# Denominators of a softmax convolution by TensorE tiles of 128 rows and 32 columns, and the gate's small matmuls in the products' tile shape

## The chip, the core and the metric

The kernel runs on one core of a Trainium2 chip. The metric is the device time of one execution in microseconds. Before the change the median of three runs is 2595.57 us.

## The reference, cut to what matters

The input has 16 images of 256 channels, 28 x 28 pixels. After a group norm two convolutions follow, each with a lookup in place of the full product, and then a squeeze-and-excitation gate:

```python
def amm_conv3x3(x, centroids, w_sub, stride=1):
    ...
    d = jnp.sum(p * p, axis=-1)[..., None] - 2.0 * jnp.einsum('bncs,cks->bnck', p, centroids) + jnp.sum(centroids * centroids, axis=-1)[None, None]
    attn = jax.nn.softmax(-d, axis=-1)
    lut = jnp.einsum('cks,cso->cko', centroids, w_sub)
    out = jnp.einsum('bnck,cko->bno', attn, lut)
...
def se_layer(x, w1, b1, w2, b2):
    s = jnp.mean(x, axis=(2, 3))
    s = jax.nn.relu(s @ w1 + b1)
    s = jax.nn.sigmoid(s @ w2 + b2)
    return x * s[:, :, None, None]
```

Two parts are touched here. The softmax has for each channel and pixel a denominator, the sum of 16 exponentials. The gate has two small matrix products for each image: 256 to 16 (the hidden layer) and 16 to 256.

## The kernel before, in words

All arithmetic is float32. The kernel does not build the big table. For each channel it first makes, from the 16 exponentials, nine weighted means (one for each tap of the 3 x 3 patch), and then multiplies these with the convolution's weights. Work goes by blocks: two layers, 16 images, and in each image four blocks (half of the channels, half of the rows of pixels), 128 blocks in all. A block has 392 pixels.

For each block TensorE does four things:

- **logits** (L607, matmuls at L616, tile `lg`): distances, by tiles of 32 rows and 32 columns, sixteen of which fill the array. They come in four portions `mm` of 16 matmuls. ScalarE turns each portion into exponentials (tile `e`, L627).
- **num_b** (L675, matmuls at L681, tile `nb`): for all four portions, a sum over the 16 exponentials of a channel with the ninth tap's centroid values (a numerator), and the plain sum (the denominator). It uses tiles of 64 rows and 32 columns. In the loop, `mm` is outermost, then the four column groups `i`, then the two row halves `r`. Row half 0 writes bank 0 of a pair of PSUM banks and row half 1 bank 1, and each bank accumulates over the four portions.
- **num_a** (L661, matmuls at L667, tile `na`): the other eight numerators, also by tiles of 64 rows and 32 columns.
- **product** (L747, matmuls at L752, tile `acc`): nine matmuls with two column halves each, by tiles of 128 rows and 64 columns (the constant `AW` is 64). The products of four blocks are combined by differences, so that seven groups of weights do the work of eight.

Rows of `nb`: in each group of 32 rows, channels that belong to row half 0 have their numerator in rows 0 to 15 and their denominator in rows 16 to 31, and the other half the other way round. `rows_of` (L84) gives the two row numbers. `split_r` (ScalarE, L691) and `join_r` (VectorE, L695) gather the denominators from the two banks into one tile `r` with the masks `m_hi` and `m_lo`; `split_q` and `join_q` (L699, L704) do the same with the numerators. `recip_dve` (L708) inverts `r`, and `spread` (L717) copies the reciprocals to the rows of each numerator with a shuffle, whose pattern is given by `mask_of` (L711). VectorE or GpSimd then multiplies (L743, L732), and GpSimd makes the differences (`mix`, L757, L761).

The order of TensorE's work is written out by hand: each job has a step number and a position, and they are sorted. In steady state there are two steps for each block, one after the other: logits, num_b, logits, a product; then logits, num_a, logits, a product. So TensorE changes from one tile shape to another four times in each step. SP's queue carries the loads of the patches (`patches`, L587, L594) for later blocks, and among them single loads of tables.

Small matmuls stand at fixed places behind a product. The group norm's (`by_cols`, L532, L534, tile `gnp`) are already done as two matmuls of 128 rows and 64 columns. The gate's hidden layer, `se_hidden` (L1038, matmuls at L1045, tile `sep`), multiplies the channel sums of an image with `w1_sb`, whose 32 columns hold the 16 hidden units twice: tiles of 128 rows and 32 columns. ScalarE adds the bias (L1047) and writes the hidden units into two columns, one for each half of the output channels (`halves`, L1049). `se_gate` (L1051, matmul at L1053) multiplies these 32 rows with `w2_sb`: one matmul of 32 rows and 128 columns. Each runs once for each of the 16 images. In the first 15 images the hidden layer is at step `g + 14` and the gate at `g + 17`, behind the product of that step, with `g` the image's first step; the last image has both at the end. The tables of the gate are loaded by `load_se` (L249, six DMAs on SP's queue) at step 92, behind the build of a table on GpSimd (`prep_cwb`, L998).

Of the kernel before, what the change touches and what calls it, by code (L numbers as in the profile page):

```python
# [8 lines left out]
F32 = mybir.dt.float32  # L9
I32 = mybir.dt.int32  # L10
U32 = mybir.dt.uint32
AF = mybir.ActivationFunctionType
ALU = mybir.AluOpType
# [4 lines left out]
P = 128  # L18
# [5 lines left out]
N = RT * W  # L24
# [56 lines left out]
AW = 64  # L81


def rows_of(m, c, a):  # L84
    r, c4, mm = c >> 1, 2 * (c & 1) + a, m & 3
    return r, c4, mm, 16 * r + 4 * mm + c4, 16 * (1 - r) + 4 * mm + c4


@with_exitstack
def kernel(  # L90
# [22 lines left out]
    nc = tc.nc  # L113
    B, C, _ = x.shape
    NB = C // P
    RED = se_w1.shape[1]

    const = ctx.enter_context(tc.tile_pool(name="const", bufs=1))
    dram = ctx.enter_context(tc.tile_pool(name="dram", bufs=1, space=DRAM))
    small = ctx.enter_context(tc.tile_pool(name="small", bufs=2))  # L120
# [12 lines left out]
    def fixed(u, kind):  # L133
        return None if u["step"] is None else EARLY.get((kind, u["step"] // 2))

    def banks(name, step=None, role=None, tag=None):
        if tag is not None:
            pass
        elif step is None:
            spin[0] = (spin[0] + 1) % 4  # L140
            tag = spin[0]
        else:
            tag = (role - step // 2) % 4
        return p_ring.tile([P, 2, 512], F32, tag=f"ps{tag}", name=name)

    def bank(name, step=None, role=None, tag=None):
        return banks(name, step, role, tag)[:, 0, :]

    def after(u, n):
        return None if u["step"] is None else u["step"] + n  # L150
# [44 lines left out]
    def load(ap, name, eng=None):  # L195
        t = const.tile(list(ap.shape), ap.dtype, name=name)
        (eng or nc.sync).dma_start(t, ap)
        return t

    wts = {}  # L200
# [37 lines left out]
        (nc.gpsimd if n in ("S2", "S4") else nc.vector).tensor_tensor(wl[n], wl[a], wl[b], op)  # L238

    vecs = load(vec, "vecs", nc.gpsimd)  # L240
    w1_sb = const.tile([P, NB, 2 * RED], F32, name="w1_sb")
    w2_sb = const.tile([2 * RED, P], F32, name="w2_sb")
    b1_sb = const.tile([2 * RED, 1], F32, name="b1_sb")
    halves = const.tile([2 * RED, NB], F32, name="halves")
    nc.gpsimd.memset(halves, 0.0)
    nc.gpsimd.memset(halves[:RED, 0:1], 1.0)
    nc.gpsimd.tensor_scalar(halves[:, 1:2], halves[:, 0:1], -1.0, 1.0, op0=ALU.mult, op1=ALU.add)

    def load_se():  # L249
        for k in range(NB):  # L250
            nc.sync.dma_start(w1_sb[:, :, k * RED : (k + 1) * RED], se_w1.rearrange("(b p) r -> p b r", p=P))
            nc.sync.dma_start(w2_sb[k * RED : (k + 1) * RED], se_w2[:, k * P : (k + 1) * P])
            nc.sync.dma_start(b1_sb[k * RED : (k + 1) * RED], se_b1.rearrange("(p o) -> p o", o=1))
# [80 lines left out]
    def small_bank(name, step, tag=None):  # L334
        return bank(name, step, step and ROLES["small"][step % 2], EARLY["small"].get(step) if tag is None else tag)
# [196 lines left out]
    def by_cols(ps, lhsT, rhs):  # L532
        for o in range(0, P, AW):
            nc.tensor.matmul(ps[o : o + AW], lhsT=lhsT[:, o : o + AW], rhs=rhs, start=True, stop=True)  # L534
# [140 lines left out]
    def num_b(u):  # L675
        bs = banks("nb", after(u, 2), ROLES["nb"], fixed(u, "nb"))
        for mm in range(4):
            es = u["e", mm]
            for i in range(4):
                for r in range(2):  # L680
                    nc.tensor.matmul(  # L681
                        bs[32 * i : 32 * i + 32, r, :N],
                        lhsT=wts["cwb", u["hh"]][64 * r : 64 * r + 64, mm, i, :],
                        rhs=es[64 * r : 64 * r + 64, i, :],
                        start=(mm == 0), stop=(mm == 3),
                    )
        u["nb"] = bs

    def split_r(u):
# [21 lines left out]
    def mask_of(k):  # L711
        if k == 8:
            return [(xx + 16) % 32 for xx in range(32)]
        mm, r = divmod(k, 2)
        return [16 * (1 - r) + 4 * mm + (xx >> 3) for xx in range(32)]

    def spread(u, mm):  # L717
        if mm == 4:
            rb = rpool.tile([P, N], F32, tag="rb1", name="rb1", bufs=1)
            nc.vector.stream_shuffle(rb, u["r"], mask_of(8))  # L720
        else:
            rb = rpool.tile([P, 2, N], F32, tag="rb", name="rb", bufs=4)
            for r in range(2):
                nc.vector.stream_shuffle(rb[:, r, :], u["r"], mask_of(2 * mm + r))  # L724
        u["rb", mm] = rb
# [310 lines left out]
    se = {}  # L1036

    def se_hidden(b, step=None, tag=None):  # L1038
        ysum = ys[b, "sum"]
        ps = small_bank("sep", step, tag)[: 2 * RED, :1]  # L1040
        terms = [(k, ysum[:, k, i : i + 1]) for k in range(NB) for i in range(2 if b >= B - 1 else 1)]
        if (b, "rest") in ys:
            terms += [(k, ys[b, "rest"][:, k : k + 1]) for k in range(NB)]
        for n, (k, term) in enumerate(terms):
            nc.tensor.matmul(ps, lhsT=w1_sb[:, k, :], rhs=term, start=n == 0, stop=n == len(terms) - 1)  # L1045
        hid = small.tile([2 * RED, 1], F32, name="se_hid")
        nc.scalar.activation(hid, ps, AF.Relu, bias=b1_sb, scale=1.0 / HW)  # L1047
        se[b] = small.tile([2 * RED, NB], F32, name="se_hh")
        nc.scalar.activation(se[b], halves, AF.Copy, scale=hid)  # L1049

    def se_gate(b, step=None, tag=None):  # L1051
        ps = small_bank("sep", step, tag)[:, :NB]
        nc.tensor.matmul(ps, lhsT=w2_sb, rhs=se[b], start=True, stop=True)  # L1053
        gt = small.tile([P, NB], F32, name="se_gt")
        for k in range(NB):
            nc.scalar.activation(
                gt[:, k : k + 1], ps[:, k : k + 1], AF.Exp, bias=nb2_sb[:, k : k + 1], scale=-1.0
            )
        nc.scalar.activation(gt, gt, AF.Identity, bias=one, scale=1.0)
        se[b] = gt  # L1060
# [179 lines left out]
    for j, u in enumerate(blocks):  # L1240
        gi, g = 8 * (j // 4), 2 * j
        for mm in range(5):
            kind = "one" if mm == 4 else "pair"
            t = g + 1 + (j > 2) if mm == 4 else g + 2 + (j > 1)
# [9 lines left out]
    for j, u in enumerate(blocks):  # L1254
# [3 lines left out]
        for p in range(2):  # L1258
# [6 lines left out]
            for q in range(2):  # L1265
                mm = 2 * p + q
# [11 lines left out]
        kept = () if j == 1 else SLOT_MM[1 : 4 if wide_next(j) or j == 0 else 2 : 2]  # L1278
        g = 2 * j + 1 + (j > 2)
        at(g, 1.0, num_b, u)  # L1280
        at(g, 1.05, split_r, u)
        at(g, 1.2 if j > 1 else 1.055, join_r, u)
# [21 lines left out]
    for l in range(2):  # L1304
        for b in range(B):
# [33 lines left out]
            if n == 2 * B - 1:  # L1339
# [14 lines left out]
                at(g + 11, 1.91, norm_out, l, b, *c22)  # L1354
                at(g + 11, 1.96, rest_sum, b, 1)
                at(g + 11, 1.98, se_hidden, b, None, 1)
                at(g + 11, 1.995, se_gate, b, None, 1)
                at(g + 12, 0.0, norm_join, b, (n, 11))
                at(g + 12, 0.01, se_recip, b)
# [39 lines left out]
            else:  # L1399
# [5 lines left out]
                if not last:  # L1405
                    at(g + 14, 2.1, se_hidden, b, g + 14)
                    at(g + 17, 2.1, se_gate, b, g + 17, 2 if near else None)
                    at(g + 18, 0.3, se_recip, b)
                    for q in range(NB):
                        if near:  # L1410
                            at(*((g + 19, 1.95) if q else (g + 18, 0.35)), gate_wide, b, q)
                            at(*((g + 19, 1.965) if q else (g + 18, 0.36)), finish_wide, b, q)
                            at(*((g + 19, 1.965) if q else (g + 18, 0.36)), store, b, q)
                            continue
                        at(g + 18, 1.9, finish_gate, b, q)
                        at(g + 20, 0.05, finish_sum, b, q)
                        at(g + 20, 1.9, finish_relu, b, q)
                        at(g + 20, 2.2, finish_add, b, q)
                        at(g + 20, 2.25, store, b, q)
# [21 lines left out]
    for o in range(2):  # L1441
# [7 lines left out]
        for part in range(2):  # L1449
            c = 40 + 8 * o + 2 * part  # L1450
# [5 lines left out]
    for part in range(3):  # L1456
        c = (68, 70, 76)[part]
# [7 lines left out]
    for part in range(4):  # L1465
        at((84, 84, 91, 92)[part], (0.5, 1.5, 2.3, 1.5)[part], prep_cwb, part)
    at(92, 2.7, prep_keep, d_cwb)
    at(92, 2.3, load_se)
    for n in range(3):
        at(96 + 8 * n, 2.6, sums_load, 3 * n)  # L1470
# [23 lines left out]
    ps = bank("gnq", tag=3)  # L1494
# [59 lines left out]
    with tc.If(rv > 0):  # L1554
        with tc.For_i(0, B, 1) as it:
            t = io.tile([P, NB, HW], F32, tag="xt", name="xt")
# [13 lines left out]
            for l in range(2):  # L1570
# [6 lines left out]
                for t2 in range(2):  # L1577
                    us = []
                    for hh in range(2):
                        u = {"l": l, "b": B, "t": t2, "hh": hh, "w": 0, "step": None}  # L1580
# [32 lines left out]
                if l == 0:  # L1613
                    for o in range(NB):
                        for r in range(2):
                            to_home2(B, o, r)
            se_hidden(B)
            se_gate(B)
            se_recip(B)
            for k in range(NB):  # L1620
# [108 lines left out]
```

## Time and profile before

| | |
|---|---|
| three runs | 2591.88, 2595.57, 2597.56 us |
| the profiled execution | 2593.79 us |
| its span, first to last instruction | 2592.0 us |
| TensorE busy | 2574.5 us |
| GpSimd, VectorE, ScalarE busy | 1911.3, 1777.4, 1372.3 us |
| granted clock of TensorE | 1.00 |

The profile is of one execution. A page of it gives busy time, the chain of work that ended last, and groups of instructions by line. A row of a group has the line, the engine, the operation, the written and the read tile, the tile shape on the array (rows\*columns), the count, the busy time, the mean length of one and the idle time before the group. Of TensorE's two rows PE is the matmuls and PEld the loads of weights. A float32 matmul stands in the records as two, so 32 matmuls of num_b are 64 instructions. Matmuls on different tiles of the array overlap, and the ends of matmuls are modelled; starts are measured. The timeline merges neighbours of the same line into one row: its start, its length from the first start to the last end, and the count.

### The profile page before, as it was taken

How to read it: one execution, taken by the hardware profiler on the slowest of the kernel's cores; microseconds unless marked ns; L12 is line 12 of the kernel's file. 1: busy time of each engine (PE TensorE's matmuls, PEld its weight loads, DVE VectorE, ACT ScalarE, POOL GpSimd, SP SyncE). 2: the span in 40 equal slices, each digit the busy share in tenths (PEclk: the TensorE clock that was granted, in tenths of full speed). 3: DMA queues.
4: the chain of work that ended last, by engine and by line, in shares of the span. 5: the costliest groups of instructions: out<-in, count | busy, mean ns of one | idle time of the engine just before them, and what ended most of it. 6: DMA issues, size and time to landing. Idle time of an engine off the chain costs nothing.

```text
span 2592.0 us, 94062 instructions
## 1 busy us (share of the span) xinstructions
PE 2574.5 (99%) x41146; PEld 1079.9 (42%) x41146; DVE 1777.4 (69%) x3797; ACT 1372.3 (53%) x1913; POOL 1911.3 (74%) x1341
## 2 busy tenths in 40 slices
PE   8999999999999999999999999999999999999998
PEld 3444444444444444444444444444444444444444
DVE  8766656666567666566676767766776667767676
ACT  6445444445445445444545555555555655555665
POOL 7687666776568776667676887878878788787786
PEclk9999999999999999999999999999999999999999
DMA  7556656665555575664664445444445444444442
GB/s 230 169 129 181 200 163 185 166 171 166 165 146 144 161 196 175 168 178 129 175 170 104 114 109 130 118 122 121 103 123 130 117 117 113 116 124 129 117 105 67
DMA packets 213321, 372.59 MB, mean 144 GB/s; under 512 B 29497, under 2 KB 183529, under 8 KB 212329
## 3 DMA queue, kind: packets, MB, share of 16 engines
q1 hardware_dynamic: 206584, 333.75, 48.3%
q0 software_dynamic: 6176, 32.66, 3.5%
q8 instruction: 327, 5.36, 0.9%
q14 instruction: 90, 0.73, 0.1%
q10 hardware_dynamic: 144, 0.10, 0.0%
HBM read 288.46 MB, written 77.95 MB: 141 GB/s over the span
## 4 chain that ended last, share of the span: by engine, by line
PE 97%; ACT 1%; POOL 1%; DVE 1%; issue 0%; DMA 0%; POOLq 0%; ACTq 0%
PE acc L752 52%; PE lg L616 17%; PE na L667 14%; PE nb L681 14%; ACT e L627 0%; POOL qp L761 0%; ACT pt L1139 0%; PE sep L1053 0%; POOL qp L732 0%; PE sep L1045 0%; DMA xt<-in_x 0%; DVE qp L743 0%; PE tap L393 0%; PE sqp L375 0%; POOL qo L732 0%
## 5 line engine op out<-in xcount | busy, mean ns | idle before, releaser
L752 PE MATMUL acc<-qp,wall 128*64 128x392 f32 x6176 | 1088.2, 494 | 1.5 <-POOL qp L761 1.2
L627 ACT ACTIVATE e<-lg 128x784 f32<-128x784 f32 x960 | 738.0, 821 | 626.5 <-PE lg L616 623.6
L761 POOL TENSOR_TENSOR qp<-qp,qp 128x784 f32<-128x784 f32 x512 | 946.2, 1871 | 148.4 <-DVE qp L743 147.9
L752 PEld LDWEIGHTS acc<-qp,wall 128*64 128x64 f32 x6176 | 424.4, 137 | 626.9 <-issue 532.0
L724 DVE STREAM_SHUFFLE rb<-r 128x392 f32<-128x392 f32 x1024 | 553.2, 607 | 0.0
L616 PE MATMUL lg<-pt,wd 32*32 32x392 f32 x15872 | 468.2, 499 | 0.5 <-issue 0.5
L695 DVE SCALAR_TENSOR_TENSOR r<-nb,kst,r 128x392 f32<-128x392 f32 x128 | 80.1, 626 | 443.8 <-ACT r L691 443.8
L667 PE MATMUL na<-e,cwa 64*32 64x392 f32 x8192 | 374.8, 492 | 0.4 <-issue 0.4
L681 PE MATMUL nb<-e,cwb 64*32 64x392 f32 x8192 | 374.7, 492 | 0.2 <-ACT e L627 0.2
L743 DVE TENSOR_TENSOR qp<-na,rb 128x784 f32<-128x784 f32 x352 | 333.9, 972 | 58.5 <-PE na L667 45.5
L732 POOL TENSOR_TENSOR qo<-qo,rb 128x392 f32<-128x392 f32 x128 | 133.0, 1039 | 289.8 <-DVE rb L720 289.6
L709 DVE RECIPROCAL r<-r 128x392 f32<-128x392 f32 x128 | 333.2, 2603 | 4.4
L732 POOL TENSOR_TENSOR qp<-qp,rb 128x784 f32<-128x784 f32 x160 | 296.8, 1865 | 2.9
L681 PEld LDWEIGHTS nb<-e,cwb 64*32 64x32 f32 x8192 | 190.7, 106 | 174.8 <-issue 21.0
L667 PEld LDWEIGHTS na<-e,cwa 64*32 64x32 f32 x8192 | 182.4, 106 | 183.9 <-issue 74.2
L616 PEld LDWEIGHTS lg<-pt,wd 32*32 32x32 f32 x15872 | 116.3, 103 | 276.7 <-issue 233.6
L752 PE MATMUL acc<-qp,w_A 128*64 128x392 f32 x1024 | 181.1, 495 | 0.0
L691 ACT ACTIVATE r<-nb,kst 128x392 f32<-128x392 f32 x128 | 86.8, 678 | 163.2 <-PE nb L681 160.1
L752 PE MATMUL acc<-qo,wall 128*64 128x392 f32 (+1 forms) x772 | 159.3, 491 | 0.1
L651 POOL TENSOR_TENSOR z<-z,mx 128x1568 f32<-128x1568 f32 x32 | 91.9, 2871 | 91.4 <-DVE mx L645 91.0
L737 ACT COPY qp<-na 128x784 f32<-128x784 f32 x160 | 130.0, 813 | 22.6 <-PE na L667 21.1
L759 POOL TENSOR_TENSOR qo<-qo,qo 128x392 f32<-128x392 f32 x128 | 131.6, 1028 | 0.1
(241 smaller groups left out, 1621.3 us busy)
## 6 DMA issues: line engine op xcount, KB each, us to landing
pt<-home SPq DMA_DIRECT2D x744, 209.0 KB
pt<-home SPq DMA_DIRECT2D x744, 104.5 KB
home<-xpad SPq DMA_DIRECT2D x30, 899.0 KB
xt<-in_x SPq DMA_DIRECT2D x30, 784.0 KB
out_dram<-y SPq DMA_DIRECT2D x31, 392.0 KB
pt<-in_p SPq DMA_DIRECT2D x6, 784.0 KB
d_wS<-st SPq DMA_DIRECT2D x12, 192.0 KB
wall<-d_wS SPq DMA_DIRECT2D x4, 576.0 KB
```

The lines of the kernel that those rows point to most:

```text
L616: nc.tensor.matmul(bk[32 * c : 32 * c + 32, :N].rearrange("p (r w) -> p r w", w=W), lhsT=(wx[u["hh"]] if early(u) else wts["wd", u["hh"]]) ...
L627: nc.scalar.activation(eg[:, 2 * i : 2 * i + 2, :], bk[:, :, :N], AF.Exp, scale=2.0)
L667: nc.tensor.matmul(bs[32 * i : 32 * i + 32, r, :N], lhsT=wts["cwa", u["hh"]][64 * r : 64 * r + 64, mm, i, :], rhs=es[64 * r : 64 * r + 64, ...
L681: nc.tensor.matmul(bs[32 * i : 32 * i + 32, r, :N], lhsT=wts["cwb", u["hh"]][64 * r : 64 * r + 64, mm, i, :], rhs=es[64 * r : 64 * r + 64, ...
L709: nc.vector.reciprocal(u["r"], u["r"])
L724: nc.vector.stream_shuffle(rb[:, r, :], u["r"], mask_of(2 * mm + r))
L732: nc.gpsimd.tensor_tensor(q, q, u.pop(("rb", mm)), ALU.mult)
L737: nc.scalar.copy(pair(u, mm), u.pop(("na", mm))[:, :, :N])
L743: nc.vector.tensor_mul(pair(u, mm), u.pop(("na", mm))[:, :, :N], rb)
L752: nc.tensor.matmul(accs[key][o : o + AW, : cols[1] - cols[0]], lhsT=wl[w][:, k, o : o + AW], rhs=us["q", k][:, cols[0] : cols[1]], start=f ...
L759: nc.gpsimd.tensor_tensor(out_u["q", 8], in0["q", 8], in1["q", 8], ALU.subtract)
L761: nc.gpsimd.tensor_tensor(pair(out_u, mm), pair(in0, mm), pair(in1, mm), ALU.subtract)
```

## The change

`num_b` uses tiles of 128 rows and 32 columns: both row halves in one matmul, 16 matmuls for a block in place of 32. Bank 0 now accumulates portions 0 and 1, and bank 1 portions 2 and 3. So that no two channels get the same row, the row numbers are dealt out anew (`rows_of`), and the shuffle patterns follow (`mask_of`).

The gate's tables are padded with zeros. `w1_sb` has 64 columns for each half of the channels, so the hidden layer's matmuls are 128\*64. `w2_sb` has 128 rows, and the hidden units stand in two fixed tiles of 128 rows in place of pool tiles of 32; the gate is done by `by_cols`, two matmuls of 128\*64. Five fills on GpSimd clear these tiles ahead of the loads in `load_se`. The room that GpSimd's DMA descriptors take in SBUF is set to 4096 bytes for each partition, which moves the tiles' addresses.

```diff
 def rows_of(m, c, a):
     r, c4, mm = c >> 1, 2 * (c & 1) + a, m & 3
-    return r, c4, mm, 16 * r + 4 * mm + c4, 16 * (1 - r) + 4 * mm + c4
+    rn = 8 * mm + 2 * c + a
+    return r, c4, mm, rn, (rn + 16) % 32
...
-    w1_sb = const.tile([P, NB, 2 * RED], F32, name="w1_sb")
-    w2_sb = const.tile([2 * RED, P], F32, name="w2_sb")
-    b1_sb = const.tile([2 * RED, 1], F32, name="b1_sb")
-    halves = const.tile([2 * RED, NB], F32, name="halves")
+    w1_sb = const.tile([P, NB, AW], F32, name="w1_sb")
+    w2_sb = const.tile([P, P], F32, name="w2_sb")
+    b1_sb = const.tile([AW, 1], F32, name="b1_sb")
+    halves = const.tile([AW, NB], F32, name="halves")
+    hidden = [const.tile([P, NB], F32, name=f"se_hh{i}") for i in range(2)]
...
     def load_se():
+        for t in (w1_sb, w2_sb, b1_sb, *hidden):
+            nc.gpsimd.memset(t, 0.0)
         for k in range(NB):
...
         for mm in range(4):
             es = u["e", mm]
             for i in range(4):
-                for r in range(2):
-                    nc.tensor.matmul(
-                        bs[32 * i : 32 * i + 32, r, :N],
-                        lhsT=wts["cwb", u["hh"]][64 * r : 64 * r + 64, mm, i, :],
-                        rhs=es[64 * r : 64 * r + 64, i, :],
-                        start=(mm == 0), stop=(mm == 3),
-                    )
+                nc.tensor.matmul(
+                    bs[32 * i : 32 * i + 32, mm >> 1, :N],
+                    lhsT=wts["cwb", u["hh"]][:, mm, i, :], rhs=es[:, i, :],
+                    start=mm % 2 == 0, stop=mm % 2 == 1,
+                )
...
         mm, r = divmod(k, 2)
-        return [16 * (1 - r) + 4 * mm + (xx >> 3) for xx in range(32)]
+        return [(8 * mm + 4 * r + (xx >> 3) + 16) % 32 for xx in range(32)]
...
-        ps = small_bank("sep", step, tag)[: 2 * RED, :1]
+        ps = small_bank("sep", step, tag)[:AW, :1]
...
-        hid = small.tile([2 * RED, 1], F32, name="se_hid")
+        hid = small.tile([AW, 1], F32, name="se_hid")
         nc.scalar.activation(hid, ps, AF.Relu, bias=b1_sb, scale=1.0 / HW)
-        se[b] = small.tile([2 * RED, NB], F32, name="se_hh")
-        nc.scalar.activation(se[b], halves, AF.Copy, scale=hid)
+        se[b] = hidden[b % 2]
+        nc.scalar.activation(se[b][:AW], halves, AF.Copy, scale=hid)
...
-        nc.tensor.matmul(ps, lhsT=w2_sb, rhs=se[b], start=True, stop=True)
+        by_cols(ps, w2_sb, se[b])
...
-    nc = _bacc.Bacc("TRN2", target_bir_lowering=False, num_devices=1)
+    nc = _bacc.Bacc("TRN2", target_bir_lowering=False, num_devices=1, dynamic_dma_scratch_size=4096)
```

More of the change, by code (lines that the diff above doesn't have):

```diff
@@ L240 @@
     vecs = load(vec, "vecs", nc.gpsimd)
-    w1_sb = const.tile([P, NB, 2 * RED], F32, name="w1_sb")
-    w2_sb = const.tile([2 * RED, P], F32, name="w2_sb")
-    b1_sb = const.tile([2 * RED, 1], F32, name="b1_sb")
-    halves = const.tile([2 * RED, NB], F32, name="halves")
+    w1_sb = const.tile([P, NB, AW], F32, name="w1_sb")
[3 more added lines that the diff above has]
+    hidden = [const.tile([P, NB], F32, name=f"se_hh{i}") for i in range(2)]
     nc.gpsimd.memset(halves, 0.0)
     nc.gpsimd.memset(halves[:RED, 0:1], 1.0)
-    nc.gpsimd.tensor_scalar(halves[:, 1:2], halves[:, 0:1], -1.0, 1.0, op0=ALU.mult, op1=ALU.add)
+    nc.gpsimd.tensor_scalar(
+        halves[: 2 * RED, 1:2], halves[: 2 * RED, 0:1], -1.0, 1.0, op0=ALU.mult, op1=ALU.add
+    )
     def load_se():
+        for t in (w1_sb, w2_sb, b1_sb, *hidden):
+            nc.gpsimd.memset(t, 0.0)
         for k in range(NB):
@@ L679, in num_b @@
             for i in range(4):
-                for r in range(2):
-                    nc.tensor.matmul(
-                        bs[32 * i : 32 * i + 32, r, :N],
-                        lhsT=wts["cwb", u["hh"]][64 * r : 64 * r + 64, mm, i, :],
-                        rhs=es[64 * r : 64 * r + 64, i, :],
-                        start=(mm == 0), stop=(mm == 3),
-                    )
+                nc.tensor.matmul(
+                    bs[32 * i : 32 * i + 32, mm >> 1, :N],
+                    lhsT=wts["cwb", u["hh"]][:, mm, i, :], rhs=es[:, i, :],
+                    start=mm % 2 == 0, stop=mm % 2 == 1,
+                )
         u["nb"] = bs
```

## The prediction

> **What bounds the kernel now.** I read the page first: the busy shares, the clock row and the chain that ended last, then the groups of TensorE.
>
> ```profile
> span 2592.0 us, 94062 instructions
> PE 2574.5 (99%) x41146; PEld 1079.9 (42%) x41146; DVE 1777.4 (69%) x3797; ACT 1372.3 (53%) x1913; POOL 1911.3 (74%) x1341
> PEclk9999999999999999999999999999999999999999
> PE 97%; ACT 1%; POOL 1%; DVE 1%; issue 0%; DMA 0%; POOLq 0%; ACTq 0%
> L752 PE MATMUL acc<-qp,wall 128*64 128x392 f32 x6176 | 1088.2, 494 | 1.5 <-POOL qp L761 1.2
> L681 PE MATMUL nb<-e,cwb 64*32 64x392 f32 x8192 | 374.7, 492 | 0.2 <-ACT e L627 0.2
> L681 PEld LDWEIGHTS nb<-e,cwb 64*32 64x32 f32 x8192 | 190.7, 106 | 174.8 <-issue 21.0
> ```
>
> TensorE is 97% of the chain, at the full granted clock in every slice, and the products (L752) and the denominators (L681) show hardly any idle time before them. What TensorE no longer does leaves the span. The edited group is L681: 374.7 us over 128 blocks, 64 instructions each (each matmul of the source stands twice in the records, so 32 matmuls). Busy time cannot say where those 2.9 us of a block go, because matmuls overlap. I therefore read starts from the timeline (start, length from first start to last end, engine, line, tiles, shape, count), over two steps in steady state:
>
> ```profile
> 1500.50 0.83 PE L752 MATMUL acc<-qo,wall 128*64 128x392 f32 x4
> 1501.26 0.29 PE L1045 MATMUL sep<-ysum,w_sb 128*32 128x1 f32 x4
> 1501.47 0.94 PE L616 MATMUL lg<-pt,wd 32*32 32x392 f32 x32
> ...
> 1506.07 1.54 PE L752 MATMUL acc<-qp,wall 128*64 128x392 f32 x8
> 1507.53 0.94 PE L616 MATMUL lg<-pt,wd 32*32 32x392 f32 x32
> 1508.40 2.92 PE L681 MATMUL nb<-e,cwb 64*32 64x392 f32 x64
> 1511.25 0.94 PE L616 MATMUL lg<-pt,wd 32*32 32x392 f32 x32
> 1512.12 4.17 PE L752 MATMUL acc<-qp,wall 128*64 128x392 f32 x24
> ...
> 1518.20 0.94 PE L616 MATMUL lg<-pt,wd 32*32 32x392 f32 x32
> ```
>
> From start to start: an acc group of 36 (rows of 24, 4 and 8) takes 1518.20 - 1512.12 = 6.08 us, one of 8 takes 1507.53 - 1506.07 = 1.46. Two 128\*64 tiles run side by side, so these are 18 and 4 passes over the array: (6.08 - 1.46) / 14 = **0.33 us a pass**, and 1.46 - 4 x 0.33 = 0.14 fixed. The nb group has 64 instructions on eight tiles, 8 passes: 1511.25 - 1508.40 = 2.85 = 8 x 0.33 + 0.21. The lg group, 32 on sixteen tiles, 2 passes: 8.40 - 7.53 = 0.87 = 2 x 0.33 + 0.21. So every group pays its passes and a fixed part, and the fixed part is what differs between shapes. The timeline cut to the starts of one first pass shows where it comes from, with the mean length of these matmuls from the groups of the same stretch behind it:
>
> ```profile
> 1508.40 0.62 PE L681 MATMUL nb<-e,cwb 64*32 64x392 f32 x8
> L681 PE MATMUL nb<-e,cwb 64*32 64x392 f32 x8 | 0.6, 512 | 0.0
> 1507.53 0.61 PE L616 MATMUL lg<-pt,wd 32*32 32x392 f32 x16
> L616 PE MATMUL lg<-pt,wd 32*32 32x392 f32 x16 | 0.6, 512 | 0.0
> 1512.12 0.55 PE L752 MATMUL acc<-qp,wall 128*64 128x392 f32 x2
> L752 PE MATMUL acc<-qp,wall 128*64 128x392 f32 x2 | 0.6, 543 | 0.0
> ```
>
> Length less one matmul is the **stagger**, from the first tile's start to the last one's. For nb 0.62 - 0.51 = 0.10 to 0.11 us over 7 steps (0.015 each), for lg 0.61 - 0.51 = 0.10 over 15 steps (0.0066 each), for acc 0.007 over one. A group ends when its last tile ends, and the next shape starts only then: the stagger is paid once in each group.
>
> **The denominators.** In place of 32 matmuls of 64\*32 a block come 16 of 128\*32. The array work is the same: 32 instructions on four tiles are again 8 passes. What goes is tiles in the stagger: four in place of eight, 3 steps in place of 7. No 128\*32 group of four tiles stands in the trace. Bounds: at the spacing of acc and lg, whose tiles follow each other by columns as the new ones do, 3 x 0.0066 = 0.02; at the spacing of 64\*32, whose order alternates between halves of the rows, 3 x 0.015 = 0.045; at worst the 0.10 stays. I take 0.02, by the two rows with the same order: **0.08 us less per block** (ends 0 and 0.085).
>
> The first and last blocks don't count. In the first 50 us TensorE is not alone on the path, and at the end it waits for GpSimd behind the last nb:
>
> ```profile
> 0.00:50.00 50.00, 41.78 (x682) 19.31 (x684) 40.42 (x114) 32.31 (x36) 31.84 (x60) 1.00 0.71 232
> 2555.06 1.54 PE L752 MATMUL acc<-qp,wall 128*64 128x392 f32 x8 [0.31 <-POOL qp L761]
> 2578.37 0.19 PE L1223 MATMUL flp<-fl 128*1 128x1 f32 x2 [0.81 <-DVE fl L1219]
> ```
>
> I count 124 of 128 blocks: 124 x 0.08 = **9.9 us**.
>
> **The gate's matmuls.** The gate (L1053, 32\*128) and its hidden layer (L1045, 128\*32) each stand between a product and an lg group, and so cost one more change of shape. A small 128\*64 matmul at the same place is already there for the group norm (gnp); here it is with the gate and a plain product:
>
> ```profile
> 1129.29 1.49 PE L752 MATMUL acc<-qp,wall 128*64 128x392 f32 x8
> 1130.61 0.23 PE L534 MATMUL gnp<-gn_mv,gmat 128*64 128x4 f32 x4
> 1130.78 0.94 PE L616 MATMUL lg<-pt,wd 32*32 32x392 f32 x32
> ...
> 1527.45 1.49 PE L752 MATMUL acc<-qp,wall 128*64 128x392 f32 x8
> 1528.87 0.38 PE L1053 MATMUL sep<-se_hh,w_sb 32*128 32x2 f32 x2
> 1529.18 0.94 PE L616 MATMUL lg<-pt,wd 32*32 32x392 f32 x32
> ```
>
> From the product's end to lg's start: gate 1529.18 - 1528.94 = 0.24, gnp 1130.78 - 1130.78 = 0.00. The new gate is gnp's form (two tiles, four instructions): 0.24 less, 14 times (images 0 to 13; the other two lie in the tail): **3.4 us**. The hidden layer has 1501.47 - 1501.33 = 0.14 now. Its four instructions stay on one tile, with twice the weight columns, so it is dearer than gnp: its group lasts 0.29 now, gnp's 0.23, and I allow once to twice that 0.06. With 0.06 to 0.12 over gnp, 0.02 to 0.08 is left; I take 0.05 x 15 = **0.7 us**.
>
> **What costs nothing.** The five fills that load_se adds run on GpSimd at step 92, and SP's six loads and all behind them (the patches) wait for them now.
>
> ```profile
> 929.92 1.01 POOL L732 TENSOR_TENSOR qo<-qo,rb 128x392 f32<-128x392 f32 x1 [6.79 <-DVE rb L720]
> 925.16 1.51 SPq L251 DMA_DIRECT2D w_sb<-in_se_w  x1
> L944 POOL MEMSET st<- 128x512 f32 x1 | 0.5, 543 | 0.0
> ```
>
> A fill of 512 columns took 0.54 us, so five of at most 128 take under 2.7. They fall in GpSimd's idle 6.79 us, from 923.1 to 929.9, and SP comes to them at 925.16: a delay of 0.7 us at most, once. Uncovered it would cost that 0.7. The masks of the shuffles and the tables change values, not sizes: nothing. Bank 0 of nb is now complete after half the group, so ScalarE's copy (L691) may start up to 1.4 us earlier; it is not on the chain. What is late next is still TensorE. The smaller scratch for descriptors concerns GpSimd's own DMAs; its price is a rival.
>
> Sum: 9.9 + 3.4 + 0.7 = **14.0 us**. The profiled execution took 2593.79 us (span 2592.0 and 1.8 around it): 2579.8. It lies 1.8 under the median of the three runs, 2595.57, which would give 2581.6; the lowest, 2591.88, gives 2577.9. I say **2580**.
>
> **The rivals.**
>
> *The stagger stays, or shrinks by half* (chance 0.16). The spacing may belong to 32 columns and not to the alternating rows, or the last tile may be held up by its weights. Then the denominators give 0 to 6.8 us (0.055 x 124), and with the gates 4 to 11: 2583 to 2590. Against it: lg, also 32 columns wide, starts its tiles 0.0066 apart.
>
> [...]
>
> *Four full-height tiles do not hide their weight loads* (0.04; slower). The place is each pass of nb. A load is 106 ns in its row; one exposed in each of 8 passes of 128 blocks adds 0.106 x 1024 = 109 us, 2689. It decides from where a pass takes over 0.33 + 14.0 / 1024 = 0.344 us. If only two of the four tiles run side by side, 8 more passes of 0.33 add 338 us, 2918. Against it: the products' weights are 128 rows high too and twice as wide, and their passes come at 0.33. For it: nowhere in the trace do four tiles of 128 rows run together.
>
> [...]
>
> *GpSimd stalls on the smaller scratch* (0.04; slower). Its indirect DMAs would wait for earlier ones to land.
>
> ```profile
> L824 POOL DMA_INDIRECT home<-hpad,col x60: 963/1011/1123, 195.4 to 1340.1; - x60
> DMA to landing us min/median/max: 3.2/5.3/9.7
> ```
>
> 60 x 5.3 = 318 us of waiting, at a GpSimd that is idle 26% of the span; if a tenth of it reached a product, 32 us: 2612. Against it: few of these transfers are in flight at once, one or two between products.
>
> *Nothing measurable comes* (0.06): another engine's wait takes the freed time, or the shape changes are paid elsewhere. 2589 to 2596. Against it: TensorE waits for POOL 1.2 us in all, and no other engine is over 74% busy.
>
> **How the numbers follow.** The forecast has 0.70. The change of run to run (2591.88 to 2597.56, less 14) puts 2578 to 2584 around it. The range reaches to the stagger rival above and 4 us under the likely case, for stagger and first-pass time that shrink more than taken: **2575 to 2590**; outside are both slow rivals, most of the "nothing" case and a little below. About 0.2%, 5.2 us, is what a measurement of this kernel can tell from no change. Faster: 0.70 + 0.14 of the stagger rival + 0.01 = 0.85. Same: the rest of that rival and 0.05 = 0.07. Slower: 0.08.
>
> **What would show it.** In the changed kernel's timeline: nb groups of 32 instructions in shape 128\*32, from start to next lg 2.77 us in place of 2.85, with a first pass of four starts over 0.02. Four instructions in shape 128\*64 at L1053's place, and lg following the product's end by about 0.00 there, by 0.06 to 0.12 behind the hidden layer. PE's count falls by 4096 less the few the gate adds, its share stays at 99%. The prediction is wrong if nb passes come farther apart than 0.33, if its fixed part stays 0.21, or if TensorE shows new idle time before qp or e.

## The result

The changed kernel takes 2580.61 us (median of 6 runs, 2577.83 to 2580.95); the kernel before 2593.5 (6 runs, 2591.88 to 2597.56). The ratio is **0.9946, with a 95% interval of 0.9934 to 0.9959**: 10.6 to 17.1 us less. The prediction on record was 2580.

The page of the changed kernel (its line numbers are up to 6 higher; L686 is the denominators, L756 the products, L622 the logits):

```profile
span 2578.8 us, 85941 instructions
PE 2561.5 (99%) x37082; PEld 1027.1 (40%) x37082; DVE 1776.3 (69%) x3797; ACT 1372.6 (53%) x1913; POOL 1911.6 (74%) x1346
PEclk9999999999999999999999999999999999999999
PE 96%; POOL 1%; DVE 1%; ACT 1%; DMA 1%; issue 0%; SPq 0%; POOLq 0%; DVEq 0%; ACTq 0%
L756 PE MATMUL acc<-qp,wall 128*64 128x392 f32 x6176 | 1088.1, 494 | 1.0 <-POOL qp L765 0.4
L686 PE MATMUL nb<-e,cwb 128*32 128x392 f32 x4096 | 366.3, 495 | 0.2 <-ACT e L633 0.2
```

Of these rows only the denominators' has changed by more than 1 us: half the instructions, 374.7 us busy before and 366.3 now. TensorE still fills 99% of the span, and the span (2592.0 to 2578.8) fell by as much as TensorE's busy time (2574.5 to 2561.5). The timeline at the place shown for the kernel before:

```profile
1494.39 0.83 PE L756 MATMUL acc<-qo,wall 128*64 128x392 f32 x4
1495.05 0.34 PE L1049 MATMUL sep<-ysum,w_sb 128*64 128x1 f32 x4
1495.32 0.94 PE L622 MATMUL lg<-pt,wd 32*32 32x392 f32 x32
...
1501.38 0.94 PE L622 MATMUL lg<-pt,wd 32*32 32x392 f32 x32
1502.25 2.86 PE L686 MATMUL nb<-e,cwb 128*32 128x392 f32 x32
1505.03 0.94 PE L622 MATMUL lg<-pt,wd 32*32 32x392 f32 x32
...
1521.23 1.49 PE L756 MATMUL acc<-qp,wall 128*64 128x392 f32 x8
1522.55 0.23 PE L540 MATMUL sep<-se_hh,w_sb 128*64 128x2 f32 x4
1522.71 0.94 PE L622 MATMUL lg<-pt,wd 32*32 32x392 f32 x32
```

From nb to the next lg it is now 1505.03 - 1502.25 = 2.78 us (2.85 before). Over all blocks the starts in the two traces give a median of 2787 ns now and 2850 before: **63 ns a block**. From the product's end to lg behind the gate it is 1522.71 - 1522.72 = -0.01 (0.24 before), and behind the hidden layer 1495.32 - 1495.22 = 0.10 (0.14 before; 638 and 594 ns from the product's last start in the traces, so 44 ns).

### The profile page after: what moved, and what is told of

Read it like the earlier page. It is cut to its first block, busy times and chain, and to the rows that moved or that the text cites. A ratio compares the mean times of both kernels' runs of the same rounds, so it can differ in the third digit from the quotient of the medians.

```text
span 2578.8 us, 85941 instructions
## 1 busy us (share of the span) xinstructions
PE 2561.5 (99%) x37082; PEld 1027.1 (40%) x37082; DVE 1776.3 (69%) x3797; ACT 1372.6 (53%) x1913; POOL 1911.6 (74%) x1346
## 4 chain that ended last, share of the span: by engine, by line
PE 96%; POOL 1%; DVE 1%; ACT 1%; DMA 1%; issue 0%; SPq 0%; POOLq 0%; DVEq 0%; ACTq 0%
PE acc L756 51%; PE lg L622 17%; PE na L673 14%; PE nb L686 13%; POOL qp L765 0%; ACT e L633 0%; DMA pt<-home 0%; ACT pt L1143 0%; POOL qp L736 0%; DVE qp L747 0%; DMA xt<-in_x 0%; POOL qo L763 0%; DMA d_sc<-score_t 0%; SPq L600 0%; PE sep L1049 0%
## 5 line engine op out<-in xcount | busy, mean ns | idle before, releaser
L756 PE MATMUL acc<-qp,wall 128*64 128x392 f32 x6176 | 1088.1, 494 | 1.0 <-POOL qp L765 0.4
L756 PEld LDWEIGHTS acc<-qp,wall 128*64 128x64 f32 x6176 | 424.3, 137 | 626.4 <-issue 529.8
L622 PE MATMUL lg<-pt,wd 32*32 32x392 f32 x15872 | 469.0, 499 | 0.6 <-DMA pt<-home 0.3
L686 PE MATMUL nb<-e,cwb 128*32 128x392 f32 x4096 | 366.3, 495 | 0.2 <-ACT e L633 0.2
L622 PEld LDWEIGHTS lg<-pt,wd 32*32 32x32 f32 x15872 | 116.1, 103 | 277.0 <-issue 235.6
L686 PEld LDWEIGHTS nb<-e,cwb 128*32 128x32 f32 x4096 | 135.0, 109 | 222.9 <-issue 155.0
L756 PE MATMUL acc<-qp,w_A 128*64 128x392 f32 x1024 | 181.1, 495 | 0.0
L756 PE MATMUL acc<-qo,wall 128*64 128x392 f32 (+1 forms) x772 | 159.2, 491 | 0.0
```

The costliest lines, as they stand in the source:

```text
L622: nc.tensor.matmul(bk[32 * c : 32 * c + 32, :N].rearrange("p (r w) -> p r w", w=W), lhsT=(wx[u["hh"]] if early(u) else wts["wd", u["hh"]]) ...
L686: nc.tensor.matmul(bs[32 * i : 32 * i + 32, mm >> 1, :N], lhsT=wts["cwb", u["hh"]][:, mm, i, :], rhs=es[:, i, :], start=mm % 2 == 0, stop= ...
L756: nc.tensor.matmul(accs[key][o : o + AW, : cols[1] - cols[0]], lhsT=wl[w][:, k, o : o + AW], rhs=us["q", k][:, cols[0] : cols[1]], start=f ...
```

## The experiments

**Three runs with one part each.** The first keeps only the edits of `num_b`, `rows_of` and `mask_of`. The second keeps only the gate's padding with the smaller scratch. The third is the kernel before with this one edit:

```diff
-    nc = _bacc.Bacc("TRN2", target_bir_lowering=False, num_devices=1)
+    nc = _bacc.Bacc("TRN2", target_bir_lowering=False, num_devices=1, dynamic_dma_scratch_size=4096)
```

> Only the denominators go by tiles of 128x32 (with the new row numbers and shuffle patterns); the gate and the scratch stay as before. Theory (the terms are separate and lie on TensorE's path): 126 blocks x 0.063 us, the difference between the traces of the two kernels in the time from nb's start to the next lg group, = 7.9 us less, ratio 0.997; nb groups as in the changed kernel, 2.79 us each; the gate's places unchanged, 0.24 us from the product's end to lg. Rival (the address shift of the scratch, or the gate, made part of what was ascribed to the denominators): under 5 us less, with nb groups of another length than in the changed kernel.

> Only the gate's small matmuls are padded (with the scratch that this needs); the denominators stay 64x32. Theory: 14 x 0.246 + 15 x 0.044 = 4.1 us less on TensorE's path, ratio 0.9984, nb groups of 2.85 us. Rival (small matmuls are hidden or their waits move on to ScalarE's gate chain): no difference, ratio 1.000, although the places themselves are shorter.

> Nothing but the smaller room for GpSimd's DMA descriptors (and so all tiles at other addresses). Theory: no difference, ratio 1.000 within 0.1%, indirect DMAs still 1.0 us on GpSimd and 5 us to landing. Rival (GpSimd stalls on the smaller room): indirect DMAs longer than 1.1 us in the median, or waits before them, and up to 30 us more time.

All ran on one chip, against a kernel before of 2591.58 us (28 runs):

| part | median, us | ratio (95% interval) | us less |
|---|---|---|---|
| denominators only | 2583.18 | 0.9966 (0.9954 to 0.9978) | 5.7 to 11.9 |
| gate only | 2587.05 | 0.9985 (0.9976 to 0.9994) | 1.6 to 6.2 |
| scratch only | 2591.93 | 0.9999 (0.9990 to 1.0008) | -2.1 to 2.6 |

The parts add up: 0.9966 x 0.9985 = 0.9951, beside 0.9946 for the whole. The first kernel's timeline, and the second's:

```profile
1502.03 2.86 PE L681 MATMUL nb<-e,cwb 128*32 128x392 f32 x32
1504.81 0.94 PE L617 MATMUL lg<-pt,wd 32*32 32x392 f32 x32
...
1522.43 0.38 PE L1052 MATMUL sep<-se_hh,w_sb 32*128 32x2 f32 x2
1522.73 0.94 PE L617 MATMUL lg<-pt,wd 32*32 32x392 f32 x32
```

```profile
1506.53 2.92 PE L686 MATMUL nb<-e,cwb 64*32 64x392 f32 x64
1509.38 0.94 PE L621 MATMUL lg<-pt,wd 32*32 32x392 f32 x32
...
1525.58 1.49 PE L757 MATMUL acc<-qp,wall 128*64 128x392 f32 x8
1526.90 0.23 PE L539 MATMUL sep<-se_hh,w_sb 128*64 128x2 f32 x4
1527.06 0.94 PE L621 MATMUL lg<-pt,wd 32*32 32x392 f32 x32
```

Each kernel has the changed kernel's interval at the place that it changes (2.78 us; -0.01 us) and the old one at the other (0.30 from the gate's start to lg's; 2.85). The rivals for the first two, that addresses or hidden waits made part of the gain, fall. In the third, GpSimd's indirect DMAs are as before:

```profile
L824 POOL DMA_INDIRECT home<-hpad,col x60: 960/1008/1122, 192.5 to 1336.8; - x60
DMA to landing us min/median/max: 3.3/5.1/9.8
```

1.01 us on GpSimd and 5.1 to landing, beside 1.01 and 5.3 before, and GpSimd waits 33.5 us in all for earlier ones to land, beside 32.2: no stall, so that rival falls too. This kernel's profiled span was 2588.8 us, 3.2 under that of the kernel before, with no edit that touches TensorE: single executions differ by that much.

**Where the spacing comes from.** The denominators gave 63 ns a block where the prediction had 80. The first pass shows it:

```profile
1502.25 0.55 PE L686 MATMUL nb<-e,cwb 128*32 128x392 f32 x4
L686 PE MATMUL nb<-e,cwb 128*32 128x392 f32 x4 | 0.6, 516 | 0.0
```

0.55 - 0.516 = 0.034, and in the starts of the trace 0, 6, 21, 38 ns: three steps of 0.0127 on average, neither the 0.0067 that the prediction took from acc and lg nor quite the 0.015 of the 64\*32 tiles. The prediction put those 0.015 down to row halves that alternate. This run turns the two loops, so that they don't:

```diff
-            for i in range(4):
-                for r in range(2):
+            for r in range(2):
+                for i in range(4):
                     nc.tensor.matmul(
```

> The kernel before with one change: num_b's loop takes the four column groups of one row half first and then those of the other, so that tiles follow each other by columns; still eight tiles of 64x32. Theory (the tiles' spacing is set by what stands ahead of the group: behind an lg group some 0.015 us a tile): first pass of nb still 0.10 us from first to last start, nb to lg 2.85 us, time as before, ratio 1.000. Rival (as the prediction had it: the spacing comes from the alternation of row halves): 7 x 0.0067 = 0.047, so 0.055 us less per block, 2.80 us, 6.8 us less in all, ratio 0.9974.

```profile
1506.94 2.92 PE L681 MATMUL nb<-e,cwb 64*32 64x392 f32 x64
1509.80 0.94 PE L616 MATMUL lg<-pt,wd 32*32 32x392 f32 x32
```

2.86 us, the starts 0, 7, 23, 40, 56, 73, 90, 106 ns, ratio 1.000 (0.999 to 1.0009). **The order of the tiles has no part in it**, and the prediction's reason falls. In the traces of this kernel and of the kernel before, a few groups start faster: behind an lg group that had to wait itself, behind two lg groups, behind a small group of another kind, or directly behind a product (in the kernel before 47, 50, 47 and 51 ns from first to last start in place of 105, at 792.07, 69.44, 20.76 and 2547.13 us). That led to groups alone, at the end of the changed kernel, where nothing has to be waited for. `lg_group(n)` are 4n tiles of 32\*32 (16 without a number), `acc_group(k)` is a product of k steps (9 without one), and `nb_group` is the denominators in 128\*32 ("full"), in 64\*32 ("half") or in 64\*32 with the loops turned ("half_outer"); none of them touches the output:

```diff
+    for rounds in range(3):
+        for before_it, kind in (
+            ((), "full"), ((lg_group,), "full"), ((), "half"), ((lg_group,), "half"), ((lg_group,), "half_outer"),
+            ((lambda: lg_group(1),), "half"), ((lg_group, lambda: acc_group(1)), "half"), ((lg_group, lambda: acc_group(1)), "full"),
+        ):
+            acc_group()
+            for f in before_it:
+                f()
+            nb_group(kind)
```

> The changed kernel with TensorE groups added behind the last product, on data that is already there and with nothing to wait for; the output is not touched by them. Eight sequences, three times: a product group (36 instructions), then nothing, an lg group of 32, an lg group of 8, or an lg group and a short product group of 4, then a denominators group of one of three kinds: four tiles of 128x32, eight of 64x32 with row halves alternating, eight of 64x32 with row halves outside. Theory (what stands ahead sets the spacing): behind the product 3 x 0.0067 = 0.02 us from first to last start for 128x32 and 7 x 0.0067 = 0.047 for 64x32; behind an lg group 0.036 and 0.10, in both orders of the loops; behind lg and a short product, or a short lg group, between the two. Rival (the shape sets it): 0.036 for 128x32 and 0.10 for alternating 64x32 whatever stands ahead, and a smaller figure for row halves outside.

The timeline of this kernel, cut to first passes: four tiles of 128\*32 behind a product and behind an lg group; eight of 64\*32 behind a product, behind an lg group with either loop order, behind an lg group of four tiles, and behind an lg group and a short product. One matmul lasts 0.51 to 0.52 us here.

```profile
2580.16 0.54 PE L1584 MATMUL bench<-qp,cwb 128*32 128x392 f32 x4
...
2589.87 0.55 PE L1584 MATMUL bench<-qp,cwb 128*32 128x392 f32 x4
...
2598.74 0.56 PE L1584 MATMUL bench<-qp,cwb 64*32 64x392 f32 x8
...
2608.48 0.62 PE L1584 MATMUL bench<-qp,cwb 64*32 64x392 f32 x8
...
2618.28 0.62 PE L1584 MATMUL bench<-qp,cwb 64*32 64x392 f32 x8
...
2627.99 0.56 PE L1584 MATMUL bench<-qp,cwb 64*32 64x392 f32 x8
...
2638.55 0.56 PE L1584 MATMUL bench<-qp,cwb 64*32 64x392 f32 x8
```

The same eight tiles are 0.56 long behind a product and 0.62 behind an lg group: 47 ns against 105 from first to last start, in all three rounds. **What stands ahead sets the spacing**, not the shape of the tiles. Four tiles of 128\*32 have 20 ns behind a product and 38 behind lg. Of the expectation, one part missed: behind a short lg group, or lg and a short product, it is not between the two but as fast as behind the product.

The next run varied what stands ahead (`lg_turned` is the lg group of 16 with its two loops turned):

```diff
         for before_it, kind in (
-            ((), "full"), ((lg_group,), "full"), ((), "half"), ((lg_group,), "half"), ((lg_group,), "half_outer"),
-            ((lambda: lg_group(1),), "half"), ((lg_group, lambda: acc_group(1)), "half"), ((lg_group, lambda: acc_group(1)), "full"),
+            ((lambda: lg_group(2),), "half"), ((lambda: lg_group(3),), "half"), ((lg_turned,), "half"),
+            ((lg_group, lg_group), "half"), ((lambda: [lg_group(1) for _ in range(4)],), "half"),
+            ((lambda: [lg_group(2) for _ in range(2)],), "half"),
```

> As the run of the groups alone, with other groups ahead of eight tiles of 64x32 (each behind a product group): lg of 16 instructions on eight tiles, of 24 on twelve, of 32 on sixteen with the loops turned, two of 32 one after the other, 32 on four tiles (four times the same four), 32 on eight tiles (twice the same eight). Theory A (TensorE's supply of instructions: a group with many short instructions drains what is queued, and the next group's come at 0.0165 us a matmul): slow, 0.10 us from first to last start, where 32 instructions pass in two passes of the array (sixteen tiles, one group or two, loops either way); 0.047 behind 16 instructions and behind four tiles, whose 32 instructions take eight passes; between for 24 on twelve. Theory B (the number of instructions of the lg shape ahead, however long they take): 0.10 in all cases with 32, also on four and eight tiles. Theory C (all sixteen tiles in use): 0.10 only with sixteen, 0.047 with twelve.

Its timeline, first pass of 64\*32 behind 8, 12 and 16 tiles, behind 16 twice, behind four tiles four times, and behind eight tiles twice (the 16 in one group are those with the loops turned):

```profile
2577.27 0.56 PE L1584 MATMUL bench<-qp,cwb 64*32 64x392 f32 x8
...
2586.98 0.58 PE L1584 MATMUL bench<-qp,cwb 64*32 64x392 f32 x8
...
2596.75 0.61 PE L1584 MATMUL bench<-qp,cwb 64*32 64x392 f32 x8
...
2607.54 0.56 PE L1584 MATMUL bench<-qp,cwb 64*32 64x392 f32 x8
...
2619.18 0.56 PE L1584 MATMUL bench<-qp,cwb 64*32 64x392 f32 x8
...
2629.54 0.56 PE L1584 MATMUL bench<-qp,cwb 64*32 64x392 f32 x8
```

None of the three theories holds as written. B falls with the last two rows, C with the second (65 ns behind twelve tiles). A had two lg groups slow, and they are fast. The starts in the trace (ns from the group's first one) say more than the lengths:

```
behind lg of  8 tiles:  0  6 13 20 26 33 40 46
behind lg of 12 tiles:  0  6 13 20 26 33 48 65
behind lg of 16 tiles:  0  9 26 43 59 76 93 109   (second round; in the first the last is at 98)
the second lg itself (17th to 20th matmul): 683 875 892 909
```

Twelve tiles and six fast matmuls, sixteen tiles and two, eight and all eight: counted from the start of the lg group, matmuls of the two groups come 6.7 ns apart up to the **18th**, and later ones 16.5. The second of two lg groups shows when the late ones come. Its first matmul (the 17th) starts at 683 ns, but its second (the 18th) at 875 and not at 690, about when the first matmul of the first group ends (its second half starts at 354, and such a half lasts 0.49 us in the trace of the changed kernel, by modelled ends). An estimate from these starts is that TensorE has **17 matmuls at hand**, counted from the oldest that is not finished. The 18th comes about when that one ends, at 875. In a denominators group that is in time, since its turn is at 871 + 7 = 878 there; the 19th comes at 892, and its turn would have been at 884. Four tiles taken four times, or eight taken twice, leave by the same estimate only their last four or eight matmuls unfinished when the denominators come (0.51 and 0.53 us long, begun 0.43 and 0.46 us ahead of them), so all eight of these are at hand. Behind a short product or a second lg group in between, the eight are fast as well, 0.56 us long. This was read from the run after the fact, so one more run tests it with numbers of tiles that no run had:

```diff
         for before_it, kind in (
-            ((lambda: lg_group(2),), "half"), ((lambda: lg_group(3),), "half"), ((lg_turned,), "half"),
...
+            ((lambda: lg_part(10),), "half"), ((lambda: lg_part(14),), "half"), ((lambda: lg_part(15),), "half"),
+            ((lambda: lg_part(14),), "full"), ((lambda: lg_part(15),), "full"),
```

> Groups alone again, to test a rule that was read from the run before: TensorE has 18 matmuls (72 records) at hand, counted from the oldest that is not finished; those beyond come one in 0.0165 us once the first of the lg group ends. Then of a denominators group behind an lg group of n tiles the first 18 - n matmuls start 0.0067 apart, and the others 0.0165. Eight tiles of 64x32 behind lg of 10 tiles: all fast, 7 x 0.0067 = 0.047 from first to last start; behind 14: four fast, 3 x 0.0067 + 4 x 0.0165 = 0.086; behind 15: three fast, 0.096. Four tiles of 128x32 behind 14: all fast, 0.020; behind 15: three fast, 2 x 0.0067 + 0.0165 = 0.030. Rival (nothing but sixteen tiles or more than twelve matters): 14 and 15 give 0.10 for 64x32 and 0.038 for 128x32, as sixteen do.

```profile
2579.73 0.56 PE L1584 MATMUL bench<-qp,cwb 64*32 64x392 f32 x8
...
2589.46 0.60 PE L1584 MATMUL bench<-qp,cwb 64*32 64x392 f32 x8
...
2599.23 0.61 PE L1584 MATMUL bench<-qp,cwb 64*32 64x392 f32 x8
...
2609.01 0.54 PE L1584 MATMUL bench<-qp,cwb 128*32 128x392 f32 x4
...
2618.72 0.54 PE L1584 MATMUL bench<-qp,cwb 128*32 128x392 f32 x4
```

These are first passes behind 10, 14 and 15 tiles, and of 128\*32 behind 14 and 15. Their starts, in the same order:

```
10, 64*32:   0  7 13 20 27 33 40 47
14, 64*32:   0  7 13 20 35 52 68 85
15, 64*32:   0  7 13 28 45 62 78 95
14, 128*32:  0  7 14 20
15, 128*32:  0  7 14 29
```

47, 85, 95, 20 and 29 ns, where the rule said 47, 86, 96, 20 and 30, and the break comes at the fifth, the fourth and the fourth matmul as it should. The rival is out. The run can't tell whether the 18th matmul is at hand from the start, as its expectation has it, or comes just in time. Counted from the first matmul of the lg group, the 18th starts at 877 or 878 ns behind 10, 14 and 15 tiles, its turn in each case, and the 19th at 892 or 893 behind 14 and 15, as behind twelve and in the second lg group of the run before. It is that second lg group, with its 18th at 875 where its turn was at 690, that speaks for 17.

## Why the prediction was right, and where a size was off

- **TensorE sets the time, and passes are not touched.** Right. The passes of four full-height tiles come 329 ns apart, as those of eight half-height ones did (starts of the first tile in the trace: 353, 682, 1012, 1341 ns). The weight loads are hidden, though loads and matmuls of all tiles share all rows:

```profile
L686 PEld LDWEIGHTS nb<-e,cwb 128*32 128x32 f32 x4096 | 135.0, 109 | 222.9 <-issue 155.0
```

  109 ns each, inside a pass of 0.33 with other matmuls in flight: in the group at 1502.25 us, counted from its first load, the loads of the second pass start at 28, 35, 47 and 64 ns and their matmuls at 355, 362, 374 and 391, while the first pass's matmuls start at 2, 8, 23 and 40 and last 0.51 to 0.52 us.
- **0.08 us a block from the stagger.** The mechanism was right, the size was not: the stagger fell from 105 to 38 ns, not to 20, and the gap from the last start to lg grew by 4 (419 to 423 ns), which leaves 63. The prediction lets the next shape start only when the last tile ends. What both traces show is a start at a fixed distance: between lg, nb, na and products, a median of 417 to 423 ns from the last start of the group ahead, 70 ns before that matmul's modelled end; the group norm's matmul, in the product's own shape, starts 323 ns from the product's last start. So the stagger is paid once in each group, as the sum has it. The step that failed is "at the spacing of acc and lg". These two were the wrong rows: lg always stands behind a long group, and acc has but two tiles, while nb stands behind lg. The third of the four tiles is the 19th matmul from the start of the lg group, the first that comes late. 126 blocks (the last two groups have no lg behind them) x 0.063 = 7.9 us, where the forecast had 9.9. The bound at 0.015 a tile, which the prediction left to a rival, was nearer in value (45 ns), and for a reason that the prediction did not have.
- **The gate, 3.4 us, and the hidden layer, 0.7.** Right in both: 14 x 0.246 = 3.4 and 15 x 0.044 = 0.7.
- **The sum.** 7.9 + 3.4 + 0.7 = 12.0 from the path; the two profiled executions differ by 2593.79 - 2580.25 = 13.5, the medians by 12.9. Most of the 1.5 us left over lies in the first layer, where waits inside a group differ from execution to execution. One such place, the same group before and after:

```profile
171.84 3.72 PE L681 MATMUL nb<-e,cwb 64*32 64x392 f32 x64
```

```profile
169.55 3.02 PE L686 MATMUL nb<-e,cwb 128*32 128x392 f32 x32
```

  Both are longer than the usual 2.92 and 2.86, one by 0.8 us and the other by 0.16. In the runs of the turned loops and of the scratch alone, which take as long as the kernel before, this group lasts 2.92, so the 0.8 us belongs to that one execution. In the second layer, from the first hidden layer (1421.3 and 1415.6 us) to the last (2577.0 and 2563.7), the lead of the changed kernel grows by 7.6 us, and the path gives 57 blocks x 0.063 + 3.4 + 0.7 = 7.7. What the rest of the 1.5 us is in each case was not tried; the third kernel's span, 3.2 us short without a cause on TensorE, shows that a single execution can differ by this much without the change. The forecast of 14.0 had 2.0 too much for the denominators, and these 1.5 us made up for most of it: that the profiled execution came so near to 2580 is in part luck.
- **The end gives nothing.** Right: TensorE still waits for the flags, and at the last products for VectorE. The gate of the fifteenth image, which the prediction did not count, stands between two products there and takes 0.32 us less (409 ns from the last start of the product ahead to the first start of the next, 731 before). A new wait for VectorE a few groups later (`pv`) takes that back.

```profile
PE flp L1227 <- DVE fl L1223: 0.7, 1, 0.7
PE pv L540 <- DVE pt L1149: 0.5, 1, 0.5
PE acc L756 <- DVE fi L1228: 0.3, 1, 0.3
```

- **What was costed at nothing.** The fills are short, and SP's first load comes as they end:

```profile
919.46 0.36 POOL L255 MEMSET w_sb<- 128x128 f32 x2
919.78 0.14 POOL L255 MEMSET se_hh<- 128x2 f32 x2
924.47 1.02 POOL L736 TENSOR_TENSOR qo<-qo,rb 128x392 f32<-128x392 f32 x1 [4.55 <-DVE rb L724]
```

```profile
919.80 1.54 SPq L257 DMA_DIRECT2D w_sb<-in_se_w  x1
```

  0.5 us in a gap of GpSimd that is 4.55 us even so. The estimate of under 2.7 us was a bound, five times the measured time, and did not matter. ScalarE's copy of bank 0 did not start earlier; it runs when the whole group is done (1505.16 us, behind an nb group whose next lg starts at 1505.03).

```profile
1505.16 0.68 ACT L695 ACTIVATE r<-nb,kst 128x392 f32<-128x392 f32 x1 [1.26 <-PE nb L686]
```

No experiment pointed to a version that beats both kernels: the late matmuls behind lg cost some 58 ns (105 - 47) wherever an nb group or one of its kind follows, but a group put in between to gain this time has a pass of its own, 329 ns. Another order of the groups was not tried.

## What to carry to other kernels

When TensorE is busy all the time (here 99% of the span), count from start to start: a group here cost its passes (0.33 us each), plus the stagger of its tiles (0.105 us for nb before, 0.038 after), plus the change of shape (the next group starts 0.42 us after the last start, 0.09 more than a pass). Fewer and larger tiles with the same number of passes saved only the stagger, 63 ns a block with the 4 ns that the gap to lg grew; small matmuls in the shape of their neighbour saved a change of shape, here 0.25 us for the gate. The hidden layer, whose four instructions stay on one tile, saved only 0.04. Take a price for the stagger from a group with the same neighbour ahead, not from a group of like shape.

## What the runs showed of the hardware that was not expected

Behind a group of 8 to 16 tiles of 32\*32 that comes after a product, matmuls of 64\*32 and 128\*32 start 6 to 9 ns apart up to the 18th from the group's start, as the 32\*32 tiles themselves do (6.7 ns); from the 19th on, at 892 or 893 ns behind 12, 14 and 15 tiles, they start 14 to 17 ns apart. The traces of both kernels have it too: behind most lg groups the first four matmuls of nb start at 870 or 871, 877 or 878, 892 or 893, and 909 or 910 ns from lg's first, before and after alike. An estimate that fits the sequences here, worked out from the second of two lg groups (its 17th matmul at 683 ns, its 18th at 875), is that TensorE has 17 matmuls of float32 at hand, counted from the oldest that is unfinished. This is read from starts alone; no run shows where they are held, nor why a matmul beyond them takes 16.5 ns.
